# Landings of two kinds of transfers counted later by a margin in a list scheduler's order

## The chip, the cores and the metric

The kernel runs on one core of a Trainium2 chip. The metric is the device time of one execution in microseconds (us), as the median of several runs. A core has five engines that matter here, each working through its own instruction stream in order: PE (matmuls, with its weight loads shown apart as PEld), DVE, ACT, POOL and SP. SP computes nothing in this kernel; it issues all the transfers (DMAs). Engines wait for each other, and for landed transfers, by semaphores.

## The reference

Four layers are applied in turn to a batch of 128 sequences of 64 tokens and 128 features. Three have causal (or plain) self-attention, cross-attention to a second input of the same shape, and an MLP; layer 1 has cross-attention with rotary positions alone. All attention has 16 heads of 8 features. Cut to what matters:

```python
def layer(x, ctx):                                   # layers 0, 2 and 3, norms before or after
    q, k, v = split_heads(ln(x) @ w_qkv)             # 16 heads of 8 features
    x = x + merge(softmax(q @ k.T * scale) @ v) @ w_o1 + b_o1
    q, (k, v) = split_heads(ln(x) @ w_q), split_heads(ctx @ w_kv)
    x = x + merge(softmax(q @ k.T * scale) @ v) @ w_o2 + b_o2
    return x + gelu(ln(x) @ w_fc1 + b_fc1) @ w_fc2 + b_fc2

def layer1(x, ctx):                                  # rotary positions on q and k
    q, k = rope(rms(x) @ w_q), rope(ctx @ w_k)
    return x + merge(softmax(q @ k.T * scale) @ (ctx @ w_v)) @ w_o

y = layer3(layer2(layer1(layer0(x, ctx), ctx), ctx), ctx)
```

## The kernel before

**Tiling and stages.** The 8192 tokens are 16 groups of 512 tokens (8 sequences), and a group is two halves of 4 sequences. Ten stages follow each other: self-attention, cross-attention and MLP of layer 0; the cross-attention of layer 1; the three of layer 2; the three of layer 3. Each stage runs over the 16 groups. x stays in on-chip memory throughout.

**One group of an attention stage.** POOL and DVE normalize x (`xn`), PE transposes it, and PE projects queries and keys into the tile `qk`, which ACT or DVE copies out of the banks of the matmul memory (in layer 1 POOL also rotates it: four instructions, lines 719 and 721). Then `plan_spread` places it: four DMAs of 128 KB (line 761) write the keys and the queries of the group into `wide`, a buffer that is zero elsewhere, so that one matmul of 32 rows works on four heads at once. This is the transfer *wide*; the scores of the group's first half are its first reader. For each half PE computes the scores (line 850), DVE takes the maximum of each row (line 877, three instructions), POOL splits the maxima into three bf16 terms (lines 905 to 908), PE turns them (line 914), ACT copies them into `ms` (line 922), and one DMA places them into `mr` (line 918). This is the transfer *mr*. Three halves later (`LAG = 3`) PE computes the transposed scores with minus the row maxima from `mr` added, ACT takes the exponentials `e` (line 885), PE averages the values with them (line 940), and ACT or DVE copies the averages into `a`. `plan_divided` then moves `a` into `z` by two pairs of DMAs (line 961, *z*), gathers the sums of the exponentials (964, *sums*), inverts them on DVE (981), and brings them back by two DMAs (967, *inv*, and 970, *spread*). POOL divides (975, `oT`), PE projects (1030) and DVE adds to x (1015).

**The order.** The order on every engine is made while the program is built, by a list scheduler, `Plan.order`. Each step is a part with an engine, a length in us, what it reads and writes, and a due time. PE's parts have due times written by hand and are run strictly in the order of these. Every other part gets its due time from its successors, backward: the earliest due time of what comes after it, less the time between, less its own length (`length`). For a DMA the length has, besides the time to issue, a landing time and a margin `lag`:

```python
def length(self, p):
    return p.us + p.lag + (self.DMA_LAG + p.kb / self.KB_US if p.engine == "SP" else 0.0)
```

Then the scheduler plays the plan forward in its own clock: whenever an engine is free it takes, of the parts that are ready, the one due first. A DMA's readers become ready when it has landed in that clock; `kb / KB_US` is its time on the shared transfer clock:

```python
if engine == "SP":
    dma_at = max(dma_at, end) + p.kb / self.KB_US
    end = dma_at + self.DMA_LAG + p.lag
```

`DMA_LAG` is 2.4 and `KB_US` 350. Without a margin a *wide* (2.5 to issue, 512 KB) counts 6.36 us from its first issue and an *mr* (0.87 to issue, 60 KB) 3.44 us. Other DMAs have margins already: 1.0 for *z* and *inv*, 1.5 for *spread*, 4.0 for *sums*. What comes out is only an order on each engine and a choice of banks. On the chip, no time of the plan is kept: every instruction starts when its engine reaches it and its semaphores are there. SP's stream stops at a DMA whose source is not ready, and everything behind it on SP stops too.

Of the kernel before, what the change touches and what calls it, by code (L numbers as in the profile page):

```python
# [56 lines left out]
CLEAR_V = 17.0, 26.0  # L57
WARM = (16, -25.0),
GATHER = 4.0
GAP = 2.6  # L60


# [34 lines left out]
    qx=3, kx=2, v=2, mr=3, mt=2,  # L97
# [21 lines left out]
class Plan:  # L119
# [22 lines left out]
    def add(self, engine, us, run, reads=(), writes=(), fresh=(), form=None, kb=0, lag=0.0, ahead=0.0, at=None, n=0, begin=0.0, or_=None):  # L142


        p = Part(engine, us, run, self.block, form)
        p.due = None if at is None else self.begins[max(0, self.block)] + at
        assert (at is None) == (engine != "PE")
        p.fresh, p.kb, p.lag, p.ahead, p.n, p.begin, p.or_ = tuple(fresh), kb, lag, ahead, n, begin, or_
        for b in reads:
            p.before.update(b.writers)  # L150
        for b in writes:
            p.before.update(b.writers, b.readers)
        for b in reads:
            b.readers.append(p)
        for b in writes:
            if b.readers:
                b.writers, b.readers = [], []
            b.writers.append(p)
        for b in (*reads, *writes):
            if b.kind:  # L160
                b.users.add(p)
        p.before.discard(p)
        for q in p.before:
            q.after.append(p)
        self.parts.append(p)
        return p
# [160 lines left out]
def kernel(ctx, tc, x, ctxT, mask, w0, w1, w2, w3, f0, f2, f3, cols, rows, consts, factors, out):  # L327
# [11 lines left out]
    def make(b, shape, dtype, name):  # L339
        if b.kind in IN_BANKS:  # L340
            at = banks[:, b.bank:b.bank + IN_BANKS[b.kind]].rearrange("p b x -> p (b x)")
            at = (at.bitcast(dtype) if dtype != F32 else at)[:, :int(np.prod(shape[1:]))]
            dims = "abcd"[:len(shape) - 1]
            b.t = at.rearrange(f"p ({' '.join(dims)}) -> p {' '.join(dims)}", **dict(zip(dims, shape[1:])))
        else:
            b.t = pools[b.kind].tile(shape, dtype, tag=b.kind, name=name)
        return b.t
# [45 lines left out]
    add = plan.add  # L393
# [5 lines left out]
    WIDE, VBDS, MRS = ([Buf() for _ in range(n)] for n in (BUFS["kx"] + BUFS["qx"], BUFS["v"], BUFS["mr"]))  # L399
# [3 lines left out]
    def wt(n, name):  # L403
        start = W_KEPT[n].index(name) * P
        return ws[n % 2][:, start:start + W_COLS[n][name]]

    def kept(n, name):
        return W[n % 2][W_KEPT[n].index(name)]
# [124 lines left out]
    def plan_mask(name, sees, reads):  # L533
# [22 lines left out]
        add("DVE", 0.5, lay_out, reads, [mt_, by_query], [mt_, by_query])  # L556
        add("PE", 0.3, turn, [mt_, IDENT], [pm], [pm, by_key], "full", at=-11.0 if name == "causal" else GAP, n=2)
        add("DVE", 0.3, lambda: nc.vector.tensor_copy(by_key.t, pm.t[:, 0:SEQ]), [pm], [by_key])
        add("PE", 0.6, put, [by_query, by_key, PICKS], [pb], [pb], "full", at=-10.0 if name == "causal" else GAP + plan.HALF, n=12)
        add("DVE", 0.8, keep, [pb, IDENT], [MASKS[name]])  # L560
# [177 lines left out]
    def place_of(kind):  # L738

        planned[kind] += 1  # L740
        return (planned[kind] - 1) % BUFS[kind]

    def next_of(kind):
        i = counts[kind] % BUFS[kind]
        counts[kind] += 1
        return i

    def plan_spread(both, k, q):

        kx, qx, placed = Buf("kx"), Buf("qx"), Buf()  # L750

        def place():
            i, j = next_of("kx"), BUFS["kx"] + next_of("qx")
            kx.t, qx.t = wide[:, i], wide[:, j]
            row = wide.ap[0][0]
            for h in range(NQ):
                to = bass.AP(
                    tensor=wide.tensor, offset=wide.offset + h * row + i * NQ * GT + h * GT,
                    ap=[[NQ * row, QUART], [(j - i) * NQ * GT, 2], [1, GT]],
                )  # L760
                nc.sync.dma_start(to, both.t[h::NQ])  # L761

        laid = [WIDE[place_of("kx")], WIDE[BUFS["kx"] + place_of("qx")]]
        add("SP", 2.5, place, [k, q, both, *laid], [placed, kx, qx], [kx, qx], kb=512)
        return kx, qx

    def quarter(k, rows=QUART):
# [46 lines left out]
    def plan_pair(new, old):  # L814
# [74 lines left out]
        if new:  # L889
            plan.block = new.block  # L890
            plan_maxima(new)
# [4 lines left out]
    def plan_maxima(f):  # L896

        d, mt, pmx, ms = Buf("d"), Buf("mt"), Buf("m"), Buf("ms")

        def split():  # L900
            mt.t = mts[next_of("mt")]
            make(d, [P, NU, NK, NQ], F32, "d")
            terms = mt.t[:, 0:3 * HEADS * NU].rearrange("p (t k i h) -> p t k i h", t=NU, k=NK, i=3)
            to = [terms[:, :, :, i] for i in range(3)]
            nc.gpsimd.tensor_copy(to[0], f.mx.t)  # L905
            nc.gpsimd.tensor_tensor(d.t, f.mx.t, to[0], ALU.subtract)
            nc.gpsimd.tensor_copy(to[1], d.t)
            nc.gpsimd.tensor_tensor(to[2], d.t, to[1], ALU.subtract)

        def turn():  # L910
            make(pmx, [P, NU, P], BF16, "pmx")
            make(ms, [3 * HEADS, TU], BF16, "ms")
            for t in range(NU):
                nc.tensor.transpose(pmx.t[:, t, :], mt.t[:, 3 * HEADS * t:3 * HEADS * t + P], ident_b)  # L914

        def place():
            f.mr.t = mrs[next_of("mr")]
            nc.sync.dma_start(f.mr.t[0:R_LAST + 1:R_STEP], ms.t)

        add("POOL", 1.1, split, [f.mx], [mt, d], [mt, d])  # L920
        add("PE", 0.15, turn, [mt, IDENTB], [pmx], [pmx, ms], "full", at=(f.u + 1) * plan.HALF + GAP - 0.2, n=4)
        add("ACT", 0.27, lambda: nc.scalar.copy(ms.t, pmx.t[0:3 * HEADS].rearrange("p t q -> p (t q)")), [pmx], [ms])  # L922
        add("SP", 0.87, place, [ms, MRS[place_of("mr")]], [f.mr], [f.mr], kb=60)

    def plan_averages(f):

# [25 lines left out]
    def plan_divided(a):  # L952
# [3 lines left out]
        def move(part):  # L956

            if part[0] == 0:
                make(z, [P, 4, TU], F32, "z")
            for i in part:  # L960
                nc.sync.dma_start(z.t[i * QUART:(i + 1) * QUART], a.t[:, i].rearrange("p u t -> p (u t)"))
# [15 lines left out]
        for part in ((0, 1), (2, 3)):  # L977
            add("SP", 1.25, lambda part=part: move(part), [a], [z, moved], [z] if part[0] == 0 else [], kb=256, lag=1.0)
        add("SP", 0.65, gather, [moved], [sums, gathered], [sums], kb=32, lag=GATHER)
        z.users.add(plan.parts[-1])  # L980
# [55 lines left out]
    def plan_value_bias(i):  # L1036
# [6 lines left out]
        def fold():  # L1043
# [4 lines left out]
        add("PE", 0.5, lambda: nc.tensor.matmul(  # L1048
            make(pb, [P, P], F32, "pb"), bv.t, wt(3, f"wo{i}"), start=True, stop=True), [bv, kept(3, f"wo{i}")], [pb], [pb], "full", at=GAP, n=4)
        add("DVE", 0.4, fold, [pb], [ROW[f"L3_bo{i}"]])  # L1050

    def plan_attention(s, g):
        n, src = s["layer"], None
        if s["cross"]:
            src = Buf("ctx")
            add("SP", 0.45, lambda: nc.sync.dma_start(
                make(src, [P, GT], F32, "ctx"), ctxT[:, g * GT:(g + 1) * GT]), writes=[src], fresh=[src], kb=256, begin=LATER)
        hT = plan_hidden(s, g, s.get("bo"), plan.when(*plan.TURN))
        src = src or hT
        bias = lambda name: col_put[:, B_PUT.index(s[name]):B_PUT.index(s[name]) + 1] if name in s else None  # L1060
        a, both = Buf("a"), Buf("qk")
        k = plan_operand(0, both, n, s["wk"], src, "rope" in s, bias("bk"), pad if s["mask"] == "cross" else None)
        q = plan_operand(1, both, n, s["wq"], hT, "rope" in s, bias("bq"), sees_any[:, 0] if s["mask"] == "self" else None)
        kx, qx = plan_spread(both, k, q)
        begun.append(kx)
        vbd = plan_values(s, src)
        block = plan.block
        given = [MASKS[s["mask"]], IDENTB] if s["mask"] else []
        for u in range(NU):
            f = types.SimpleNamespace(  # L1070
                s=s, g=g, u=u, block=block, mask=s["mask"], both=both, kx=kx, qx=qx, vbd=vbd, a=a,
                given=[k, q, *given], mx=Buf("mx"), mr=Buf("mr"), es=[Buf("e"), Buf("e")],
            )
            halves_on.append(f)
            plan_pair(f, halves_on.popleft() if len(halves_on) > LAG else None)
# [309 lines left out]
```

## Time and profile before

| | us |
|---|---|
| three runs | 1709.56, 1715.78, 1714.78 |
| median of the three | 1714.78 |
| the profiled execution, its own time | 1710.07 |
| its span, first to last instruction | 1708.1 |

The stages take these stretches of the span, with the busy time of some engines (from a table of windows; the borders are read from the first and last matmuls of each stage, to a few us):

| stage | stretch, us | length | PE busy | POOL busy | DMA share |
|---|---|---|---|---|---|
| layer 0 self | 22 to 222 | 200 | 188.10 | 132.81 | 0.46 |
| layer 0 cross | 222 to 394 | 172 | 165.94 | 110.83 | 0.52 |
| layer 0 MLP | 394 to 520 | 126 | 124.43 | 84.65 | 0.14 |
| layer 1 cross | 520 to 704 | 184 | 175.43 | 143.23 | 0.47 |
| layer 2 self | 704 to 909 | 205 | 197.31 | 109.61 | 0.42 |
| layer 2 cross | 909 to 1087 | 178 | 173.39 | 145.59 | 0.51 |
| layer 2 MLP | 1087 to 1226 | 139 | 132.60 | 123.41 | 0.14 |
| layer 3 self | 1226 to 1406 | 180 | 173.28 | 145.45 | 0.39 |
| layer 3 cross | 1406 to 1579 | 173 | 168.61 | 118.85 | 0.53 |
| layer 3 MLP | 1579 to 1708 | 129 | 123.49 | 61.60 | 0.21 |

How to read the views shown below: the view of waits has one line for each pair of waiter and releaser ("who, which line, waited for whom: us in total, times, longest"). The chain of waits is followed back from the last instruction, at each step to what released it. The timeline gives start, length, engine and line, and in brackets the idle time before. "q" after an engine's name is its sequencer, so SPq L918 is the issue of the *mr* transfer.

### The profile page before, as it was taken

Reading aid. Unit: us, or ns where it says so; the run is one execution under the profiler, and the core shown is the slowest. Engines: PE = TensorE matmul, PEld = TensorE weight load, DVE = VectorE, ACT = ScalarE, POOL = GpSimd, SP = SyncE. Lnnn points to the kernel's source line nnn. Section 1 sums busy time; section 2 is a strip of 40 time slices with the busy share of each in tenths; the row PEclk is TensorE's granted clock in tenths of the full one; section 3 lists DMA queues with packets and bytes.
Section 4 is the critical chain, followed back from the end, with each engine's and each line's share of the span. In section 5 each row is a group of like instructions: output and inputs, shape, how many; then the busy total and the mean of one; then the engine's idle time right before and its main releaser. Section 6 shows DMA issues by size and latency. Waiting matters only on the chain.

```text
span 1708.1 us, 87778 instructions
## 1 busy us (share of the span) xinstructions
PE 1638.8 (96%) x38243; PEld 1258.5 (74%) x38243; DVE 1162.2 (68%) x2758; ACT 1198.7 (70%) x1789; POOL 1186.0 (69%) x1912
## 2 busy tenths in 40 slices
PE   7999999999999999999999999999899999999999
PEld 4677777767996676777777766799667777777898
DVE  7667676675557777556666767566799987778452
ACT  7777777877445777777777777844387877777643
POOL 4666766666768887436558886899778887657570
PEclk9999999999999999999999999999899999999999
DMA  4444355553003455544444555310124445554311
GB/s 148 131 141 138 115 149 147 152 158 80 13 11 102 135 154 149 146 120 122 118 124 134 147 154 143 92 28 7 45 98 133 134 133 146 156 162 141 72 45 44
DMA packets 194624, 195.05 MB, mean 114 GB/s; under 512 B 53952, under 2 KB 142144, under 8 KB 194240
## 3 DMA queue, kind: packets, MB, share of 16 engines
q1 hardware_dynamic: 194240, 189.45, 38.4%
q8 instruction: 300, 4.92, 1.3%
q14 instruction: 84, 0.69, 0.1%
HBM read 25.51 MB, written 4.19 MB: 17 GB/s over the span
## 4 chain that ended last, share of the span: by engine, by line
PE 73%; POOL 6%; DVE 6%; DMA 5%; issue 3%; ACT 3%; SPq 3%; POOLq 0%; DVEq 0%; ACTq 0%
PE banks L850 26%; PE banks L940 11%; PE banks L704 9%; PE banks L1121 8%; PE banks L1108 6%; PE banks L1030 5%; PE banks L997 4%; PE banks L653 3%; DVE mx L877 3%; PE banks L914 2%; ACT e L885 2%; DMA wide<-qk 2%; DMA mr<-ms 2%; POOL xn L620 1%; SPq L761 1%
## 5 line engine op out<-in xcount | busy, mean ns | idle before, releaser
L877 DVE TENSOR_REDUCE mx<-banks 128x8 f32<-128x512 f32 (+1 forms) x672 | 548.6, 861 | 256.6 <-PE banks L850 245.9
L850 PE MATMUL banks<-wide,qk 32*64 32x256 f32 x14336 | 540.1, 381 | 21.9 <-issue 16.0
L885 ACT ACTIVATE e<-banks 128x512 f32<-128x512 f32 (+1 forms) x576 | 391.6, 739 | 149.3 <-PE banks L850 146.6
L850 PEld LDWEIGHTS banks<-wide,qk 32*64 32x64 f32 x14336 | 346.6, 132 | 92.6 <-issue 36.8
L940 PEld LDWEIGHTS banks<-e,v 128*32 128x32 f32 x14336 | 212.8, 110 | 102.8 <-issue 79.6
L1002 ACT COPY v<-banks 64x512 f32<-64x512 f32 x224 | 247.1, 1103 | 33.0 <-PE banks L997 31.4
L940 PE MATMUL banks<-e,v 128*32 128x64 f32 x14336 | 250.1, 221 | 6.4 <-ACT e L885 5.5
L684 POOL TENSOR_TENSOR x<-x,row_sb 128x512 f32<-128x512 f32 x144 | 185.4, 1293 | 54.4 <-PE banks L653 52.3
L1113 ACT ACTIVATE h<-banks,col_sb 128x512 f32<-128x512 f32 x192 | 126.3, 688 | 120.4 <-PE banks L1108 82.5
L1121 PEld LDWEIGHTS banks<-w,h 128*128 128x128 f32 x1536 | 190.6, 192 | 15.3 <-issue 3.9
L1121 PE MATMUL banks<-w,h 128*128 128x128 f32 x1536 | 197.5, 276 | 3.2 <-ACT ms L922 3.1
L947 ACT COPY a<-banks 128x512 f32<-128x512 f32 x221 | 129.5, 586 | 95.6 <-PE banks L940 92.4
L620 POOL TENSOR_TENSOR xn<-x,mv 128x512 f32<-128x512 f32 x109 | 118.0, 1083 | 99.0 <-PE banks L653 93.3
L975 POOL TENSOR_TENSOR oT<-z 128x512 f32<-128x512 f32 x112 | 144.0, 1285 | 51.9 <-DMA z<-inv 17.1
L613 POOL TENSOR_TENSOR rstd<-rstd,nhalf 128x4 f32<-128x4 f32 x160 | 166.9, 1043 | 13.4
L704 PE MATMUL banks<-turned,wp 128*128 128x512 f32 x320 | 163.5, 604 | 2.7 <-ACT turned L578 1.7
L905 POOL CAST mt<-mx 128x32 bf16<-128x32 f32 x224 | 47.5, 212 | 145.9 <-DVE mx L877 143.8
L598 DVE BATCH_NORM_STATS2 st<-x 128x6 f32<-128x128 f32 x640 | 139.0, 277 | 10.7 <-POOL x L664 5.2
L850 PE MATMUL banks<-mr,minus 32*64 32x512 bf16 x1280 | 129.4, 388 | 5.1 <-DMA mr<-ms 4.5
L1030 PE MATMUL banks<-w,oT 128*128 128x128 f32 x896 | 119.4, 276 | 1.2 <-issue 1.2
L620 POOL TENSOR_TENSOR xn<-xn,rstd 128x512 f32<-128x512 f32 x109 | 115.3, 1058 | 5.7
L1030 PEld LDWEIGHTS banks<-w,oT 128*128 128x128 f32 x896 | 109.5, 192 | 2.8 <-issue 1.3
(121 smaller groups left out, 2563.3 us busy)
## 6 DMA issues: line engine op xcount, KB each, us to landing
wide<-qk SPq DMA_DIRECT2D x448, 128.0 KB
z<-a SPq DMA_DIRECT2D x448, 128.0 KB
z<-inv SPq DMA_DIRECT2D x112, 256.0 KB
ctx<-in_ctxT_dram SPq DMA_DIRECT2D x64, 256.0 KB
mr<-ms SPq DMA_DIRECT2D x224, 24.0 KB
x<-in_x_dram SPq DMA_DIRECT2D x16, 256.0 KB
out_dram<-x SPq DMA_DIRECT2D x16, 256.0 KB
sums<-z SPq DMA_DIRECT2D x112, 32.0 KB
```

The costliest lines, as they stand in the source:

```text
L613: nc.gpsimd.tensor_tensor(r, r, nhalf, ALU.pow)
L620: nc.gpsimd.tensor_tensor(xn.t, xg if step == 0 else xn.t, by_, ALU.subtract if mean else ALU.mult)
L684: add("POOL", 1.28, lambda: nc.gpsimd.tensor_tensor(xg, xg, row(out_bias), ALU.add), [ROW[out_bias]], [X[g]])
L704: nc.tensor.matmul(a.t, w, src.t, start=True, stop=True)
L850: nc.tensor.matmul(m[0], m[1], m[2], start=m[3], stop=m[4])
L877: add("DVE", (1.15 if step else 0.61), lambda b=b, k=k, n=2 // len(sc[step]): nc.vector.tensor_reduce(new.mx.t[:, :, k:k + n].rearrange("p ...
L885: add("ACT", 0.5 if n == 1 else 0.95, lambda b=b, to=e, n=n, i=i: nc.scalar.activation(to.t[:, i:i + n].rearrange("p i h n q -> p (i h n q ...
L940: nc.tensor.matmul(av.t[j * VO:(j + 1) * VO, i, h * SEQ:(h + 1) * SEQ], f.vbd.t[:, 2 * f.u + h, v], f.es[i // 2].t[:, i % 2, h, j], start= ...
L975: nc.gpsimd.tensor_tensor(oT.t.rearrange("p t c q -> p c t q"), x, r, ALU.mult)
L1002: copy(vbd.t[half, :, :, c::4], pv.t[half])
L1030: nc.tensor.matmul(po.t[:, t, :], oT.t[:, t].rearrange("p c q -> p (c q)"), wo, start=True, stop=True)
L1121: nc.tensor.matmul(po.t[:, t, :], hs[k // 2].t[:, k % 2, t * P:(t + 1) * P], fc2[:, k * P:(k + 1) * P], start=k == t == 0, stop=k == NC4 - ...
```

## The change

A constant is added, and the two `add` calls that plan *wide* and *mr* get it as their margin. Nothing that is computed, no transfer and no buffer is changed.

```diff
 GATHER = 4.0
+PLACE = 1.5
 GAP = 2.6
@@ plan_spread
-        add("SP", 2.5, place, [k, q, both, *laid], [placed, kx, qx], [kx, qx], kb=512)
+        add("SP", 2.5, place, [k, q, both, *laid], [placed, kx, qx], [kx, qx], kb=512, lag=PLACE)
@@ plan_maxima
-        add("SP", 0.87, place, [ms, MRS[place_of("mr")]], [f.mr], [f.mr], kb=60)
+        add("SP", 0.87, place, [ms, MRS[place_of("mr")]], [f.mr], [f.mr], kb=60, lag=PLACE)
```

The length counted for a *wide* becomes 7.86 us and for an *mr* 4.94 us, so both and what feeds them are due 1.5 us earlier, and in the plan's clock their readers are ready 1.5 us later.

The two built programs have the same instructions, and compared engine by engine their orders stand so (groups are numbered 0 to 111 over the seven attention stages, 16 to a stage; "a" and "b" are a group's halves):

| engine | difference |
|---|---|
| PE | none: 11266 rows (equal neighbours merged) in both, in the same order; the banks that the tiles take are others |
| ACT | one swap in the first 20 us (a clearing of a buffer goes ahead of the copy of a transposed x) |
| SP, start | a 256 KB and a 64 KB load of weights move ahead of the *mr* of half 1a, a 0.5 KB load of biases ahead of the *wide* of group 3; ahead of the *wide* of group 4 small loads change places |
| SP, layer 0 self | ahead of the *wide* of groups 7 to 12, `x mr` becomes `mr x` (x is the load of a later group's input, 256 KB) |
| SP, layer 0 cross | ahead of the *wide* of groups 24 to 31, `mr sums z inv ctx mr z spread` or `mr z inv sums ctx mr z spread` becomes `mr inv z sums ctx mr spread z` |
| SP, layer 1 | between two *wide*, `z mr inv mr ctx sums z spread` becomes `mr z inv sums mr ctx z spread` ahead of the *wide* of groups 39, 41, 43 and 45, and stays in those between; once (group 39) a second *mr* goes ahead of the *wide* |
| SP, layer 2 | ahead of the *wide* of groups 56 to 79 as in layer 0 cross |
| SP, layer 3 | none, up to the last group's tail |
| DVE | in most groups of layer 2 and some of layers 0 and 1 the inversion (981) comes after the third maximum of a half (877) or ahead of line 1015, where it stood one place off; in places means and variances (598, 603) move past one or two neighbours |
| POOL, layers 0 cross and 2 cross | in 22 groups the division `oT` moves ahead of one or both steps of `xn` (620), with one reciprocal root (612, 613) past a split of the maxima in some; in four groups of layer 2 self ahead of a reciprocal root |
| POOL, layer 1 | the reciprocal roots (608 to 613) of later groups, which stood ahead of the rotations (719, 721) in groups 38 to 42, are earlier by some groups or stand behind the rotations |
| POOL, layer 3 | one `xn` step moved at the end of the cross-attention |

## The prediction

> **What bounds the kernel now.** I read the busy times first, then the chain of waits, then the waits stage by stage, and last the SP queue beside PE in one group.
>
> ```profile
> span 1708.1 us, 87778 instructions
> PE 1638.8 (96%) x38243; PEld 1258.5 (74%) x38243; DVE 1162.2 (68%) x2758; ACT 1198.7 (70%) x1789; POOL 1186.0 (69%) x1912
> ...
> PE 73%; POOL 6%; DVE 6%; DMA 5%; issue 3%; ACT 3%; SPq 3%; POOLq 0%; DVEq 0%; ACTq 0%
> ```
>
> PE is busy for 1638.8 of 1708.1 us, and its instructions and their order stay as they are. What the change can win is therefore within the 69.3 us in which PE stands, and only the part of it that waits on *wide* and *mr* is aimed at. Over the whole span the view of waits has:
>
> ```profile
> PEld L850 <- DMA mr<-ms: 10.9, 17, 1.7
> ...
> PE banks L850 <- DMA wide<-qk: 4.5, 9, 1.1
> PE banks L850 <- DMA mr<-ms: 4.5, 6, 1.3
> ```
>
> 9.0 us of standing matmuls and 10.9 us of standing weight loads, which overlap in part: 9 to 20 us. A second way to size it: for the first matmul of each half that reads a newly landed *wide* or *mr*, I took from the timeline the time since the matmul before it, less that of an undisturbed half of the stage. That gives by stage: layer 1 6.0 us on *mr* and 1.3 on *wide*; layer 0 cross 1.7 and 1.6; layer 3 cross 1.9 and 2.6; about 2 in the rest. Together 17 us, 1.0% of the run, and this is the ceiling. The same waits in the window of layer 1 (520 to 704):
>
> ```profile
> PE banks L850 <- DMA mr<-ms: 2.7, 4, 1.2
> ...
> PEld L850 <- DMA mr<-ms: 6.8, 10, 1.7
> ```
>
> More than a third of the ceiling lies in this one stage of 184 us. Why, one of its groups shows (chain of waits):
>
> ```profile
> 648.89 1.28 SPq L761
> ...
> 651.56 0.58 SPq L961
> ...
> 652.83 3.51 DMA mr<-ms
> 656.34 0.04 issue
> 656.38 2.13 PE banks L850 x63
> ```
>
> The maxima were in `ms` at 646.74 (end of ACT's line 922), but SP was first busy with *wide* (648.21 to 651.5, it had waited for POOL's rotation) and a pair of *z*, so *mr* went out at 652.83, 6.1 us later, and PE took it 0.04 us after it landed. In layer 1, 11 of 32 *mr* are met within 0.2 us of landing, all of the b halves; the median from `ms` to issue is 2.96 us and from issue to landing 2.45. In layer 3 cross 8 of 32 are that tight (median to issue 3.43), in layer 0 cross 2, in layer 2 none: there the median slack from landing to use is 4.4 to 4.6 us.
>
> **The change, part by part.** It adds no work: 448 and 224 DMAs stay, each as large. All it does is the other order.
>
> *Layer 1, where the waits are.* In every second group *mr* b passes one pair of *z*, 1.23 us of issue in the rows above (651.56 to 652.83), and often a short wait of that pair for `a`. The *mr* concerned stand, by my per-half list, for 0.09, 0.88, 0.32, 0.21 and 1.62 us; each becomes shorter by at least 1.2 us, so 0.09 + 0.88 + 0.32 + 0.21 + 1.2 = 2.7 to 3.1 us go. The other tight b halves (0.44, 0.50, 0.73, 0.09, 0.92, 0.32: 3.0 us) keep their place behind *z*. They can gain through POOL: *wide* waits for the rotations, and the reciprocal root that stood ahead of these costs 8.3 + 1.8 + 1.6 + 1.6 = 13.3 us for 8 groups, 1.66 us each. In some five groups it is now off that path, which brings *wide*, *z* and *mr* forward by up to 1.66 us. Ends: 0 (something else holds the rotations) and 3.0 + 1.3 (all that is left of both kinds). I take 2.5, nearer the upper end, since the chain in this stage runs through POOL, rotations and *wide*. Together 2.9 + 2.5 = 5.4 us off. What is late next is the exponentials (line 940 waits for ACT 2.3 us there) and the maxima (0.4). Passed over are the *z* pair and *sums*, later by one *mr*, 0.87 us; `oT` is ready 4.9 us or more before PE reads it in this stage, which covers it. Once an *mr* goes ahead of a *wide* whose slack was 0.38 us: 0.87 − 0.38 = 0.5 us back.
>
> *Layer 0 cross and layer 2.* *inv* and *spread* each pass other DMAs, *sums* and one *z* pair fall back. *mr* and *wide* have as many DMAs ahead of them as before, and so keep their times: the waits of layer 0 cross (3.3 us) stay, and layer 2 had 0.3 (one *wide*). I take 0. On POOL `oT` is now ahead of two steps of `xn` (1083 and 1058 ns). In layer 2 cross it began a median 2.48 us after *spread* had landed; 2.14 of that go, and *spread*, issued ahead of a *z* pair, comes 1.2 us sooner: it still fits. `xn` falls back by the 1285 ns of `oT`; its transposes come 6 us or more after it in most groups of layer 2 cross and 6.9 in layer 0 cross: covered. The third maximum is up to 541 ns sooner (the inversion's length), but a split of the maxima is done 1.9 to 3.6 us before PE turns it, so it gains nothing.
>
> *Layer 0 self and the start.* `mr x` for `x mr` brings *mr* forward by one issue of x (0.51 us) or its wait (up to 1.77), in a stage with one tight *mr*: nothing. x lands 0.85 us later for 6 groups; DVE has waited for it 3.6 us in 4 places. Ends 0 and 6 × 0.85 = 5.1; DVE is busy for 65% of the stage, so I take 1.0 back. At the start 320 KB pass the *mr* of half 1a: two issues (0.33 to 0.63 us each) and 320 KB at the 148 GB/s of that slice, 2.2 us, together some 3.2, less its slack of 2.34: 0.9 back at most. A mask load that DVE was held up by (the chain has 3.43 us of it, ending at 52.29) is issued one or two places sooner, 0.6 to 1.3. I take 0.
>
> *Layer 3 and the MLPs.* SP is the same, so its 4.5 us of tight landings stay: 0.
>
> **Where a rule speaks against it.** By the rows of this trace an *mr* lands 2.0 us after its issue at the least, 2.06 to 3.04 as the stages' medians, 6.79 at most; a *wide* lands 5.3 to 6.0 us after its first issue (medians), 7.25 at most. The plan counted 3.44 (2.57 of it after the issue) and 6.36 already, so the margin fits the worst landings and not the usual ones. The Trainium skill, "DMA: Bandwidth & Descriptors", section "Anatomy of one DMA", fits a DMA by a fixed cost of about 2.0 us and its bytes over 436 GB/s (for another issuing path). By it a margin has nothing to cover and the sum would be 0; by the rows the time lost is ahead of the issue, in the queue, which only a changed order mends, and the sum is what layer 1 gives.
>
> **The sum.** −5.4 + 0.5 + 1.0 = −3.9, with the smaller *wide* waits left as they are: about −4 us. The profiled execution took 1710.07 (span 1708.1 and 2.0 around it), below the median of the three, 1714.78; the difference carries over to the median: 1714.78 − 4 = 1710.8. The ends of this case: −8 (−5.4 − 1.8 more in layer 1, −0.8 of the mask load) and 0 (2.7 in layer 1 less 0.5, 1.0 and 0.9), so 1707 to 1715.
>
> **Rivals.** *More goes than I see.* `mr` 5.4 in layer 1 with all of its 7.3, the 3.3 of layer 0 cross if *wide* there stops waiting behind a *spread* that waits for *inv* (it went out as little as 0.02 us after *inv* had landed), and some of the 8.4 us in which line 914 waits for DVE, of which 1.7 are in layer 0 cross and 3.5 in layer 0 self: 7.3 + 3.3 + 2 to 5 = −13 to −16, 1699 to 1702. For it: the same order in every group of layer 2 and a POOL that is freer. Against: layer 3 keeps its waits.
>
> *Given back.* x, the start and the *wide* behind an *mr* cost 1.0 to 5.1, 0.9 and 0.5, and layer 1 gives only 2.7: −0.3 to +3.8, 1714.5 to 1718.5.
>
> *Slower: instruction blocks arrive later.* The profile has
>
> ```profile
> q8 instruction: 300, 4.92, 1.3%
> ...
> PE banks L850 <- issue: 19.0, 25, 3.3
> ```
>
> 300 blocks of 16 KB are fetched by the DMA engines that carry the data, and at nearly every one of these 25 waits a block had landed 1.2 to 1.6 us before PE went on: PE runs out of instructions. Layer 2 self has 6.7 us of it in 9 waits, layer 2 cross 2.8 in 4. There *spread* (256 KB), a *z* pair (256 KB) and *wide* (512 KB) follow each other in another order, and fetches may meet them worse. If each of the 24 changed groups of layer 2 and the 8 of layer 0 cross lost one such wait of 0.75 us (6.7 / 9) it would be 24.0, against 9.5 + 1.2 now: +13, and with layer 1's gain +9 to +13, 1724 to 1728. It decides from some 12 more waits. Against it: the bytes between two *wide* stay the same. The skill's "Runtime: NRT & Kernel Launch", section "Instruction fetch mechanics", calls fetching hidden by the dispatch; by it this rival would be 0, but the row of 19.0 us disagrees.
>
> *The margin does nothing.* PE's order is the same, and layer 3 shows that whole stages stay; it goes with "given back".
>
> **How the numbers follow.** Forecast 0.46 (0.05 of it under −8.6), more 0.24, given back 0.14, slower 0.16. 0.5% of the median is 8.6 us, about what a measurement of this kernel can tell from no change (its three runs span 6.2). Faster by more: 0.05 + 0.24 = 0.29; within: 0.41 + 0.14 = 0.55; slower: 0.16. The range 1698 to 1722 takes in the forecast, nearly all of "more" and "given back", and leaves out most of "slower"; the forecast's own is 1707 to 1715.
>
> **What would show it.** In layer 1's window the PEld row on *mr* falls from 6.8 us to under 4, its stretch from 184 to about 179; layer 3's waits on *mr* and *wide* (0.6, 2.2 on PE; 2.3 on PEld) stay as they are; layers 0 cross and 2 stay within 2 us each; `oT` does not wait longer for *spread*. I am wrong if layer 1 keeps its waits, or if layer 2 moves by more than 3 us in either direction.

## The result and the profile after

| | before | changed |
|---|---|---|
| runs on the same chip | 15 | 15 |
| median, us | 1709.52 | 1718.80 |
| range, us | 1703.81 to 1715.78 | 1712.76 to 1728.11 |
| the profiled execution, us | 1710.07 | 1722.72 |
| its span, us | 1708.1 | 1720.9 |

The changed kernel is slower: the ratio is 1.0052, with a 95% interval of 1.0037 to 1.0068, or 9 us where I forecast 4 us less. The range of 1698 to 1722 holds the time, partly by luck: it was laid around 1714.78, the median of three runs, and the fifteen have 1709.52. The direction was wrong.

The changed kernel's line numbers are one higher than before's (L851 for L850, L919 for L918). The first lines of its page and of its chain:

```profile
span 1720.9 us, 87771 instructions
PE 1640.7 (95%) x38243; PEld 1262.0 (73%) x38243; DVE 1164.3 (68%) x2758; ACT 1198.8 (70%) x1789; POOL 1186.1 (69%) x1912
...
PE 72%; POOL 8%; DMA 5%; DVE 4%; issue 4%; SPq 4%; ACT 3%; POOLq 0%; DVEq 0%; ACTq 0%
```

PE's work is the same (1640.7 against 1638.8 us); it stands 80.2 us instead of 69.3. Whole-run waits of PE and PEld:

```profile
PE banks L851 <- issue: 18.3, 21, 3.6
PE banks L915 <- DVE mx L878: 12.2, 11, 3.9
PE banks L851 <- DMA mr<-ms: 7.6, 13, 1.1
PE banks L851 <- DMA wide<-qk: 7.3, 8, 1.7
...
PEld L851 <- DMA mr<-ms: 14.9, 17, 1.5
```

The waits that the margin was aimed at grew: *mr* from 4.5 to 7.6 us, *wide* from 4.5 to 7.3, the weight loads' from 10.9 to 14.9. The waits for DVE grew from 7.3 to 12.2. The fetch of instructions (19.0 before) did not grow in this pair.

PE runs the same 38243 matmuls in the same order in both, so the traces can be laid on each other matmul by matmul. A stretch below runs from the first matmul that before started in it to the first of the next:

| stretch of before, us | before | changed | difference |
|---|---|---|---|
| start and layer 0 self, 0 to 222 | 220.2 | 221.5 | +1.4 |
| layer 0 cross, 222 to 394 | 172.0 | 181.1 | +9.1 |
| layer 0 MLP, 394 to 520 | 126.1 | 126.1 | 0.0 |
| layer 1, 520 to 704 | 184.0 | 189.8 | +5.8 |
| layer 2 self and cross, 704 to 1087 | 383.1 | 382.2 | -0.9 |
| layer 2 MLP, 1087 to 1226 | 139.0 | 135.7 | -3.3 |
| layer 3, 1226 to the end | 477.7 | 478.1 | +0.4 |

Together 12.5 of the 12.8 us between the spans. The loss sits in two stages, and three findings in the trace name its pieces.

**Layer 0 cross: SP.** The waits of PE and of PEld in this stage (223 to 404 us of the changed execution):

```profile
PE banks L851 <- DMA wide<-qk: 4.6, 3, 1.7
PE banks L851 <- DMA mr<-ms: 3.2, 6, 1.1
...
PEld L851 <- DMA mr<-ms: 6.3, 7, 1.5
```

Before had 1.4, 1.3 and 1.7 there. Why they land later, SP's timeline shows for one group, from one *wide* to the next:

```profile
373.43 3.76 SPq L762 DMA_DIRECT2D wide<-qk  x4
377.29 0.83 SPq L919 DMA_DIRECT2D mr<-ms  x1
378.22 0.58 SPq L968 DMA_DIRECT2D inv<-sums  x1
378.91 1.73 SPq L962 DMA_DIRECT2D z<-a  x2
380.69 0.59 SPq L965 DMA_DIRECT2D sums<-z  x1
381.38 0.83 SPq L919 DMA_DIRECT2D mr<-ms  x1
382.31 1.59 SPq L971 DMA_DIRECT2D z<-inv  x1
383.95 1.42 SPq L962 DMA_DIRECT2D z<-a  x2
385.48 3.10 SPq L762 DMA_DIRECT2D wide<-qk  x3
```

Before had for the same group:

```profile
364.54 2.57 SPq L761 DMA_DIRECT2D wide<-qk  x4
367.21 0.90 SPq L918 DMA_DIRECT2D mr<-ms  x1
368.21 0.58 SPq L964 DMA_DIRECT2D sums<-z  x1
368.88 1.25 SPq L961 DMA_DIRECT2D z<-a  x2
370.22 0.56 SPq L967 DMA_DIRECT2D inv<-sums  x1
370.87 1.55 SPq L918 DMA_DIRECT2D mr<-ms  x1
372.48 1.22 SPq L961 DMA_DIRECT2D z<-a  x2
373.80 0.58 SPq L970 DMA_DIRECT2D z<-inv  x1
374.56 3.69 SPq L761 DMA_DIRECT2D wide<-qk  x4
```

From one *wide* to the next it is 10.02 us before and 12.05 changed. There is no rest between the changed rows beyond the 0.05 to 0.11 us from one issue to the next: SP is always issuing or standing at an issue whose source is not there. A *wide* takes 2.57 when nothing holds it, a pair of *z* 1.23, *spread* 0.58; in the changed rows they take 3.76, 1.73 and 1.42, and 1.59. To see what that leaves, I counted each issue between the *wide* of group 24 and that of group 31 at the shortest length usual for its kind (the lower tenth: 0.59 for one of the four of *wide*, 0.81 *mr*, 0.58 one of *z*) and called the rest of it a wait. Per group before: 8.50 of issues, 1.30 between them, 1.23 of waits, 11.03 in all. Changed: 8.50, 1.15 and 2.69, 12.34 in all. A group that PE runs undisturbed takes 10.72 in this stage. So SP needs 9.7 of 10.7 us for its issues and the time between them, and the room for waits is about 1 us per group.

**Layer 1: a load of weights.** The chain of waits around the longest stall of the stage:

```profile
668.28 3.48 DMA put<-in_w_dram
671.77 0.02 issue
671.79 0.04 DVE wp L439
...
672.25 0.61 DVE mx L878
672.86 0.04 issue
672.90 0.37 PE banks L915 x2
```

SP issues the two loads of layer 2's weights (`put`, line 429 of before) some 8 us later in relation to PE than before (667.69 against 646.85 us, of which 12.8 are the delay of all), on the other side of a *wide*. DVE keeps the place of the copy that reads them, stands there 4.7 us, and the maxima behind it are late: PE stands 3.9 us.

**Layer 1: a root.** The chain 125 us earlier, where PE stands 1.8 us:

```profile
546.64 1.04 POOL rstd L614
547.67 0.18 POOL mt L906
...
548.85 0.40 PE banks L915 x2
```

A reciprocal root (545.74 to 547.68) now stands ahead of the split of the maxima. It left the way of the rotations, as the prediction had it, and got into another.

**Behind the stalls: the clock.** The rows of layer 1, before and changed (stretch, length, busy time of PE, PEld, DVE, ACT and POOL with their instructions, granted clock, DMA share, GB/s):

```profile
520.00:704.00 184.00, 175.43 (x4552) 124.69 (x4550) 137.65 (x267) 130.86 (x200) 143.23 (x244) 1.00 0.47 137
530.00:720.00 190.00, 176.57 (x4553) 126.24 (x4553) 138.22 (x267) 131.24 (x200) 143.11 (x244) 0.97 0.46 133
```

In the changed execution the granted clock is 0.50 from 548.6 to 552.0 and from 671.4 to 678.2 us, right behind the two stalls, and full in the rest of the stage; before has it full throughout. Half of these 10.2 us, 5.1, is an estimate of the matmul time lost; against it and the stalls stands the weight loads' wait for *mr*, which fell by 2.8 us. In layer 0 cross one such stretch follows a wait for *wide* (391.6 to 395.0; 1.7 of the 9.1 us by the same estimate). In the MLP of layer 2 before has one (1201.1 to 1207.9; 3.4 us) and the changed kernel none. Over the twenty traces, 109 of 110 such stretches begin right behind 3.4 us in which PE was busy for at most 0.7. A long stall of PE can cost more than its own length here.

### The profile page after: what moved, and what is told of

Its sections match the earlier page's. It is cut to its first block, busy times and chain, and to the rows that moved or that the text cites. A ratio compares the mean times of both kernels' runs of the same rounds, so it can differ in the third digit from the quotient of the medians.

```text
span 1720.9 us, 87771 instructions
## 1 busy us (share of the span) xinstructions
PE 1640.7 (95%) x38243; PEld 1262.0 (73%) x38243; DVE 1164.3 (68%) x2758; ACT 1198.8 (70%) x1789; POOL 1186.1 (69%) x1912
## 4 chain that ended last, share of the span: by engine, by line
PE 72%; POOL 8%; DMA 5%; DVE 4%; issue 4%; SPq 4%; ACT 3%; POOLq 0%; DVEq 0%; ACTq 0%
PE banks L851 25%; PE banks L941 11%; PE banks L705 9%; PE banks L1122 7%; PE banks L1109 5%; PE banks L998 5%; PE banks L1031 5%; PE banks L654 3%; PE banks L915 2%; DMA mr<-ms 2%; ACT e L886 2%; POOL xn L621 2%; SPq L762 2%; DVE mx L878 2%; DMA wide<-qk 1%
## 5 line engine op out<-in xcount | busy, mean ns | idle before, releaser
L851 PE MATMUL banks<-wide,qk 32*64 32x256 f32 x14336 | 541.9, 381 | 27.0 <-issue 15.5
L851 PEld LDWEIGHTS banks<-wide,qk 32*64 32x64 f32 x14336 | 348.3, 131 | 94.2 <-issue 36.6
L851 PE MATMUL banks<-mr,minus 32*64 32x512 bf16 x1280 | 130.0, 390 | 8.5 <-DMA mr<-ms 7.6
```

The source lines that it names most:

```text
L851: nc.tensor.matmul(m[0], m[1], m[2], start=m[3], stop=m[4])
```

## The experiments

Most of them are hybrids. The kernel plans twice, with the margin at 0 and at 1.5, which gives `old` and `new`, the lists of steps of each engine. It then builds the list `take` of each engine from the two and plays the plan a third time with every engine but PE, whose order is fixed, bound to its list. `as_in(a, b, part)` keeps the places that the steps of `part` have in `a` and fills them in the order of `b`; `between(sp, i, j)` are SP's steps from *wide* number i to number j, counted from 0. The hybrids keep before's line numbers. Ratios are to before on the same chip, with 95% intervals. Stage lengths are of one profiled execution each, by the matmuls of the table above, and several executions with the same order in a stage serve as one another's measure. A few diffs below are sketches of SP's order ahead of one *wide*, written with the names of the transfers.

### SP's order in layer 0 cross

Into before, and out of the changed kernel (`b_sp`, `a_sp`):

```diff
 take = dict(old)
+take["SP"] = as_in(old["SP"], new["SP"], between(old["SP"], 23, 33))
```
```diff
 take = dict(new)
+take["SP"] = as_in(new["SP"], old["SP"], between(new["SP"], 23, 33))
```

> The orders of before on every engine, and of the change only SP's order between the wide of group 23 and that of group 33 (layer 0 cross). Theory A (in this stage SP itself is nearly full, and 'mr inv z sums ctx mr spread z' makes it wait longer, so mr and wide land later): the stage goes from 172.0 us to 179 to 182, the run becomes 7 to 10 us longer than before (ratio 1.004 to 1.006), and the other stages stay within 2 us. Rival B (the order of POOL or DVE in that stage, or the other banks of the matmul memory, made the loss): the stage stays at 171 to 174 and the run within 2 us of before.

> The orders of the changed kernel on every engine, except SP's order between the wide of group 23 and that of group 33, which is that of before. Theory A: layer 0 cross goes back from 181.1 us to 171 to 174 and the run loses 7 to 10 us, to a ratio of 0.999 to 1.002 to before. Rival B (POOL, DVE, banks): the stage stays near 181 and the ratio near 1.005.

`b_sp`: 178.7 us for the stage, ratio 1.0026 (1.0001 to 1.0051). `a_sp`: 174.0, ratio 1.0035 (1.0012 to 1.0058). The stage follows SP's order both ways, 6.7 us in and 7.1 out; the whole follows it by about half of that, within the intervals, and both ratios lie outside what theory A expected.

The two pieces of that order, each alone (`b_spr`, `b_inv`; in some of the groups before has `z inv sums` for `sums z inv`):

```diff
-mr sums z inv ctx mr z spread WIDE
+mr sums z inv ctx mr spread z WIDE
```
```diff
-mr sums z inv ctx mr z spread WIDE
+mr inv z sums ctx mr z spread WIDE
```

> The orders of before; of the changed order only one piece, in layer 0 cross ahead of the wide of groups 24 to 31: spread goes ahead of the pair of z that it followed. Theory A1 (the harm is here: the pair of z, which waits for the averages, now stands directly ahead of wide): layer 0 cross from 172 to 177 to 181 us. Theory A2 (the harm is in inv ahead of z and sums): the stage at 171 to 174.

> The orders of before; of the changed order only the other piece, ahead of the wide of groups 24 to 31: 'mr inv z sums ctx mr' for 'mr sums z inv ctx mr' or 'mr z inv sums ctx mr', with z spread as before. Theory A2: layer 0 cross from 172 to 176 to 181 us; theory A1: 171 to 174. If both pieces cost some 3 us, the harm is in each place that SP stops.

`b_spr`: 179.3 us, ratio 1.0041 (1.0016 to 1.0066). `b_inv`: 176.2, ratio 1.0007 (0.9982 to 1.0033). The swap of *spread* and *z* is enough for the whole loss; the other piece shows 3 us over the mean of before's order in the stage (see below) and nothing that can be told in the total.

Is it that SP is full? `b_load` adds issues to before in a full stage and in a freer one, `a_act` takes one off SP in the changed kernel:

```diff
     for p in plan.order():
         p.run()
+        wides += p.kb == 512
+        if p.engine == "SP" and (p.kb == 512 or p.kb == 256 and p.us == 0.65) and (wides in range(25, 33) or wides in range(57, 65)):
+            more = 8 - more
+            nc.sync.dma_start(pads[:, more:more + 8], rows[:, more:more + 8])
```
```diff
-            add("SP", 0.45, lambda: nc.sync.dma_start(
+            add("SP", 0.45, lambda: (nc.scalar if n == 0 and g in range(7, 16) else nc.sync).dma_start(
```

> Before, with two more tiny loads (32 bytes each, some 0.55 us of SP and 0.1 between) after each wide and each spread of groups 24 to 31 (layer 0 cross) and 56 to 63 (layer 2 self). Theory A (in layer 0 cross SP works 9.8 us of a group whose floor on PE is 10.7, in layer 2 self 9.1 of 12.4): layer 0 cross gets 3 to 10 us longer (at most 8 x 1.3), layer 2 self stays within its spread of 2 us. Rival (SP has room everywhere, what counts is only which wait stands ahead of what): both within 2 us.

> The changed kernel, with the loads of ctx for groups 23 to 31 (layer 0 cross) issued by ACT instead of SP: some 0.55 us and a wait of up to 1.8 us less on SP in each group, and the changed order of all other issues kept. Theory A (SP is full there and late, and everything that it issues is late with it): layer 0 cross goes from 177 to 181 us (four executions with this order) to 172 to 176, and fewer mr are met at their landing. Rival (it is the pair of z directly ahead of wide that waits, whatever else SP does): the stage stays at 177 to 181.

`b_load`: layer 0 cross 179.8 us, layer 2 self 202.7 where twelve executions with before's order there have a mean of 202.6; ratio 1.0029 (1.0002 to 1.0057). Two loads of 32 bytes per group cost over 6 us in one stage and nothing in the other. `a_act`: 175.3, against 177.4 to 181.1 with the changed order on SP. Its waits of PE in the stage:

```profile
PE banks L850 <- ACT a L947: 2.1, 4, 0.7
PE banks L850 <- DMA wide<-qk: 1.1, 1, 1.1
PE banks L850 <- DMA mr<-ms: 1.0, 1, 1.0
```

*wide* and *mr* wait 1.1 and 1.0 us in place of 4.6 and 3.2, and 2 of 32 *mr* are met within 0.2 us of landing where the changed kernel has 12; ACT, which now issues, gives 2.1 back. Over the whole run no gain shows (1.0053, 1.0027 to 1.0079; one of 4 us would lie at the edge of this): layers 1 and 2 keep the changed order and were long in the profiled execution (190.8 and 389.5).

So theory A holds, with one limit. Twelve executions with before's order on SP in this stage have 169.7 to 177.7 us (mean 173.4), and two of the twelve are as long as the changed ones (177.4 to 181.1, mean 178.7, four executions). Before's order can fall behind as well; the changed order does so each time.

Much of that width is one group's. From the fourth to the fifth output projection of the stage (271.8 to 285.0 us of before), where SP's order is the same in all but `a_act`, the twenty executions take 12.2 to 16.9 us, whatever order follows. Without it the stage has 157.0 to 163.5 (mean 159.5) with before's order and 161.7 to 167.2 (mean 163.3) with the changed one, 164.7 in `b_spr`, 167.5 in `b_load`, but 160.2 in `b_inv` and 159.3 in `a_act`. So the 3 us of `b_inv` are not its piece's, one issue less per group on SP brings the stage back whole (one execution each), and the changed order costs nearer to 4 us than to 5.

### Layer 1

The loads of weights back at their places (`a_w`):

```diff
-z mr inv mr ctx sums z spread WIDE44 ... sums put put mr ctx z spread put put WIDE45
+z mr inv mr ctx sums z spread put put WIDE44 ... sums put put mr ctx z spread WIDE45
```

> The orders of the changed kernel, except that the two loads of layer 2's weights (put, line 429) are back at their old places on SP in layer 1, ahead of the wide of group 44 instead of behind it. Theory A2 (DVE stands at line 438 until the load has landed, and the maxima behind it with it): the wait of 4.2 us ahead of line 914 near 670 us goes, layer 1 goes from 189.8 us to 185.5 to 187, and the run becomes 3 to 4.5 us shorter than the changed kernel (ratio to before 1.002 to 1.004). Rival: the wait is only seen in this execution, or the maxima are late for another reason: layer 1 stays at 189 to 191 and the ratio at 1.005.

Layer 1 took 183.3 us, at full granted clock; PE no longer waits for DVE's maxima in the stage. The changed order with the loads at their new places has 185.2, 189.8 and 190.8 (`a_sp`, the changed kernel, `a_act`; mean 188.6). Ratio 1.0040 (1.0017 to 1.0062): the stage is as expected and better, the total at the edge of it, with layer 0 self at its longest in this execution (226.3 to its end).

SP's order alone, and POOL's alone, in stages that lie apart (`b_l0_l1`, `b_pool_l2`):

```diff
 take = dict(old)
+for lo, hi in ((1, 13), (36, 46)):
+    take["SP"] = as_in(take["SP"], new["SP"], [p for p in between(old["SP"], lo, hi) if p.kb != 128])
```
```diff
 take = dict(old)
+take["POOL"] = as_in(old["POOL"], new["POOL"], [p for p in old["POOL"] if 49 <= p.block < 65])
+take["SP"] = as_in(old["SP"], new["SP"], between(old["SP"], 55, 79))
```

> The orders of before, with SP's order from the changed kernel in two stages that lie apart: ahead of the wide of groups 3 to 12 (layer 0 self) and of groups 37 to 45 (layer 1), the weight loads left where they were. Layer 1: if SP's order alone brings the gain seen between 600 and 660 us (58.8 to 60.6 us for that stretch in before's order, 56.1 to 57.8 with the changed order), that stretch takes 56 to 58 and the stage some 3 us less than 184; if the roots' places on POOL bring it, 60 and 184. Layer 0 self: with before's order six executions took 196.9 to 201.2 us, with the changed one three took 201.2 to 205.9; if SP's order does that, 201 to 206, if not, 197 to 201.

> The orders of before, with two pieces of the changed one in stages that lie apart: POOL's order in layer 1 (a reciprocal root goes ahead of the split of the maxima in the first groups) and SP's order in layer 2 ahead of the wide of groups 56 to 79 (the same swaps as in layer 0 cross). Layer 1: line 914 waits 1.6 to 1.9 us for POOL early in the stage, which gets that much longer in its first 20 us. Layer 2: by theory A (mr and wide have 4 us of slack here, and SP is less full) self and cross stay within 2 us of the means of before's order, 203.3 and 176.0; by the rival (the swaps cost wherever they are made) each gets 5 us or more longer.

`b_l0_l1`: layer 1 took 183.9 us (before's order: 183.4 to 186.7, mean 184.7, ten executions), the stretch of 600 to 660 us some 2 less than the mean of before's order and the 20 us behind it 1.4 more. Up to 222 us it took 219.4: SP's `mr x` costs nothing. Ratio 0.9999 (0.998 to 1.0018). SP's order in layer 1 alone brings no gain that can be told. `b_pool_l2`: layer 1 took 188.1, and its waits have

```profile
PE banks L914 <- POOL mt L908: 3.7, 3, 1.8
```

where before has 0.4. POOL's order costs 3 us in layer 1 beside before's order on SP (188.2 in `b_eng`, below). Beside the changed order on SP it does not: `a_w` has it, with 2.3 us of these waits, and took 183.3. So the two orders are not worth what each is worth alone; these are single executions.

### Layer 2

`b_pool_l2` has 383.6 us for layer 2 self and cross, and a ratio of 1.0043 (1.0024 to 1.0063). That is neither the 2 us of theory A nor the 10 of its rival. So its two pieces were taken apart, the same swaps as above, ahead of the *wide* of groups 56 to 79:

> Before, and in layer 2 ahead of the wide of groups 56 to 79 spread goes ahead of the pair of z. Layer 2 self and cross together took 374 to 383 us (mean 377.7) in nine executions with before's order there, 382 to 386 (mean 383.2) in five with the changed one. If this swap does it: 382 to 386, with PE's waits for instructions in layer 2 self at 6 to 10 us (3.8 to 6.9 with before's order); if not, 374 to 380.

> Before, and in layer 2 ahead of the wide of groups 56 to 79 the other piece, inv ahead of z and sums. If this does it: self and cross together 382 to 386 us, PE's waits for instructions in layer 2 self 6 to 10; if not, 374 to 380. If both pieces stay low, the loss needs both.

`b_l2_spr`: 383.8 us, ratio 1.0027 (1.0004 to 1.005). `b_l2_inv`: 388.1, ratio 1.0041 (1.002 to 1.0062). `b_eng`, below, with before's order on SP and run with them: 379.2. Over all profiled executions the two stages took 377.8 with before's order (374.0 to 383.1, twelve) and 384.2 with the changed one (382.2 to 389.5, six). Before's own profiled execution is the longest of its twelve, which is why the pair above shows nothing here. The pieces alone stand 5 and 9 us above `b_eng`. In the twelve, PE waits for instructions 3.8 to 7.3 us in layer 2 self (mean 5.7), in the six 5.8 to 9.5 (mean 8.0): 2.3 of the 6.4 us. The waits of `wide_only` (before's order on SP there) and of `b_pool_l2` in that stage:

```profile
PE banks L850 <- issue: 3.6, 8, 0.9
```
```profile
PE banks L850 <- issue: 7.8, 9, 1.6
```

`b_l2_spr` has only 5.4 of it, though, with its loss in layer 2 cross, where 5.1 us of landings of *mr* stand. `b_l2_inv` has 5.2, and 3.2 and 3.5 us of waits of line 850 for ACT's line 947 in the two stages. So each execution loses in another place, and what the rest is made of is not settled.

### Each margin alone

```diff
-        add("SP", 2.5, place, [k, q, both, *laid], [placed, kx, qx], [kx, qx], kb=512, lag=PLACE)
+        add("SP", 2.5, place, [k, q, both, *laid], [placed, kx, qx], [kx, qx], kb=512)
```
```diff
-        add("SP", 0.87, place, [ms, MRS[place_of("mr")]], [f.mr], [f.mr], kb=60, lag=PLACE)
+        add("SP", 0.87, place, [ms, MRS[place_of("mr")]], [f.mr], [f.mr], kb=60)
```

The first is `mr_only`, the second `wide_only`.

> The margin on mr alone. By the built order SP goes in layers 0 cross and 2 as in the changed kernel and the weight loads of layer 2 stay where before had them, the first pair ahead of the wide of group 44. Theory A: layer 0 cross 177 to 181 us, layer 1 within 3 us of 184, the run 1.002 to 1.005 of before. Rival (the two margins act together, or wide's is the harmful one): layer 0 cross near 172, the run within 2 us of before.

> The margin on wide alone. By the built order SP goes in layer 0 cross as before, and the weight loads of layer 2 go out a group later as in the changed kernel. Theory A: layer 0 cross 171 to 174 us; in layer 1 DVE stands for the weights and line 914 waits 2 to 4 us near 660 us, the stage 185 to 188; the run 1.000 to 1.004 of before. Rival (each margin does the whole harm): layer 0 cross near 179.

`mr_only`: layer 0 cross 177.5, layer 1 183.7, layer 2 385.5 us; ratio 1.0025 (0.9991 to 1.0058). `wide_only`: layer 0 cross 169.7, layer 1 186.0, layer 2 374.6; ratio 0.9991 (0.9972 to 1.001). The margin on *mr* is what turns SP's order round in layers 0 cross and 2. That on *wide* moves the loads of weights (DVE stood 2.8 us for them, PE 1.6) and costs nothing that can be told. Layer 0 cross and the total of `wide_only` came out below what theory A expected, and the interval of `mr_only` still holds no change.

### The other engines, the banks, and the best of both

`b_banks` is before in every order, with the banks of the margin's clock; `b_eng` has the changed orders on DVE, ACT and POOL and before's on SP; `b_eng_l0` and `b_eng_l2` have these only in layer 0 self and only from layer 2 on; `best` takes what seemed good.

```diff
-return play(plan, 0.0, old)
+return play(plan, PLACE, old)
```
```diff
-take = dict(new)
+take = dict(new, SP=old["SP"])
```
```diff
 take = dict(old)
+for e in ("DVE", "ACT", "POOL"):
+    take[e] = as_in(old[e], new[e], [p for p in old[e] if p.block < 17])
```
```diff
 take = dict(new)
+take["POOL"] = as_in(new["POOL"], old["POOL"], [p for p in new["POOL"] if 49 <= p.block < 65])
+take["SP"] = as_in(old["SP"], new["SP"], [p for p in between(old["SP"], 36, 46) if p.kb != 128])
```

> The orders of before on every engine, but the banks of the matmul memory chosen in the plan's clock with the margin counted, so that most matmul outputs lie where the changed kernel has them. Theory A (only orders matter): within 2 us of before, every stage within 2 us. Rival C (the other banks, by letting ACT or DVE hold PE up, made part of the loss): up to 1.005, with layer 0 cross or layer 1 3 us or more longer.

> SP's order of before, the changed orders on DVE, ACT and POOL, and their banks. Theory: layer 0 cross 170 to 175 us, layer 2 374 to 380, layer 1 1.9 us longer at its start for the root on POOL (186 to 188), the stretch from 1087 to 1226 at 136 to 137.5 instead of 138.8; the run within 0.998 to 1.002 of before. Rival (the other engines' orders make part of the loss beyond layer 1): 1.003 or more, seen in a stage's length.

> Before, with the changed orders of DVE, ACT and POOL among the steps of layer 0 self alone. If the moved statistics and maxima on DVE cost the time there: the stretch up to 222 us takes 222 to 226 us (nine executions with before's orders: 218.8 to 221.6), the run some 2 to 5 us more than before, 1.001 to 1.003. If the longer executions were the clock's or the fetches' doing: 219 to 222, and within 0.999 to 1.001.

> Before, with the changed orders of DVE, ACT and POOL from layer 2 on, SP's as before. Theory: the stretch from 1087 to 1226 takes 136.5 to 137.5 us instead of 138.7, layer 2 374 to 380, all else as before: 1 to 3 us under before, a ratio of 0.998 to 1.000, which would make it the fastest version, by less than can be told with certainty. Rival: 1.001 or more.

> What the runs say is good in the changed order, alone: its orders on DVE and ACT, on POOL outside layer 1, and SP's order ahead of the wide of groups 37 to 45 with the weight loads at their old places; SP elsewhere and POOL in layer 1 as before. Theory A: layer 0 cross 171 to 174, layer 1 181 to 183, the stretch from 1087 to 1226 2 to 3 us shorter than before's 138.8: 4 to 7 us under before, a ratio of 0.996 to 0.998. Rival (the gains come only together with the losses): 0.999 to 1.002.

`b_banks`: 1.0004 (0.9981 to 1.0027), no stage over 1 us longer than in before: the banks are not it. `b_eng`: 1.0011 (0.9987 to 1.0036), 224.0 us up to the end of layer 0 self. `b_eng_l0`: 223.6 there, 1.0019 (1.0001 to 1.0036): the moved statistics and maxima cost 3 us, as far as can be told (before's orders 218.8 to 221.6, mean 220.1, eleven executions; these orders 221.5 to 226.3, mean 223.9, seven). Of the 3.8 between the means, 2.7 go with the granted clock: stretches at 0.50 cost an estimated 5.8 us in the seven and 3.1 in the eleven. Whether the orders bring these stretches on is not shown. `b_eng_l2`: PE's wait for line 1045 in the MLP of layer 2 is 1.6 us, as with these orders in all eight executions that have them there (1.6 to 1.8) and in none of the twelve others (4.6 to 4.7). The stage took 138.2 all the same, above what I expected, with the granted clock at 0.50 in its last 5 us; ratio 1.0003 (0.998 to 1.0025). `best`: 1.003 (1.0009 to 1.005), slower than before, against my expectation; it kept the orders that `b_eng_l0` shows to cost (225.6 up to 222). No version was shown to be faster than before.

The stages' means do not add up to the whole: 3.8 (layer 0 self), 5.3, 3.9 (layer 1), 6.4 and −2.0 (MLP of layer 2) make 17 us, and the medians of fifteen runs differ by 9.3 (6.3 to 11.6). The profiled executions show where time goes, and not its shares.

## Why the prediction was wrong

**The step that failed.** "*mr* and *wide* have as many DMAs ahead of them as before, and so keep their times" in layers 0 cross and 2, priced at 0. The number of DMAs ahead is the same; how long SP stands at them is not, and I did not count how full SP was. In layer 0 cross it is full to about 1 us per group, and a stall in a full queue is passed on to all behind it. It cost 9.1 us in the pair, 5.3 in the means of sixteen executions, 3.8 without the group that no moved issue reaches. In layer 2 I called the landings covered by 4.4 to 4.6 us of slack; the means say 6.4 us lost, of which 2.3 are the fetch of instructions; what the rest is stays open.

**Layer 1, -5.4 + 0.5.** The mechanism was there: the weight loads that wait for *mr* fell from 6.8 to 4.0 us. But PE's own wait fell only from 2.7 to 2.1, and three things stood up in its place: the root ahead of a split (PE's wait on POOL 0.4 to 2.3), the load of weights (3.9), *wide* (0.6 to 1.9). Behind the first two the granted clock was 0.50 for 10.2 us, some 5 us by the estimate above, and the sum had no term for that. The 2.5 that I gave to roots moved out of the rotations' way is a loss of some 3 in `b_pool_l2` (none in `a_w`): I named where the roots left and not where they went. The load of weights moved past a *wide* I did not price at all: DVE has a fixed place for what reads it.

**Layer 0 self, +1.0 for x behind *mr*.** SP's swap costs nothing (`b_l0_l1`), yet 3 to 4 us are lost, with the order on DVE, ACT and POOL (`b_eng_l0`; 1.4 in the pair), much of it as granted clock. I had looked at DVE's moved statistics and given them no price.

**Layer 3 as before.** Right: +0.4 us.

**The MLP of layer 2.** Not in the sum, and 3.3 us shorter in the pair, 138.7 to 136.7 in the means: PE's wait for DVE's line 1045 falls from 4.7 to 1.6 us, as the load of layer 3's weights goes out sooner, and the stretch at half clock behind the longer wait (3.4 us by the estimate) is gone; 1.4 come back as a wait of line 850 for DVE. It comes with the orders of DVE, ACT and POOL (`b_eng_l2`), not with SP's (4.6 in `b_pool_l2`). Which of their moved steps does it was not found.

**The rivals.** "Given back" had the direction, with at most 3.8 of the 9 us, and not the places: x behind *mr* cost nothing. The one on the slower side, more fetches that come late, is about a third of what happened in layer 2 and next to none of it in layer 0 cross (1.5 us before, 1.8 changed). "The margin does nothing" and "more goes" are out.

**The rule on fetches.** The Trainium skill's "Runtime: NRT & Kernel Launch", section "Instruction fetch mechanics", calls them mostly hidden. By their number they are, with 25 waits before at 300 blocks; but they are 19.0 us of PE's standing before and 18.3 after, and in layer 2 self they vary from 3.8 to 9.5 between executions. For SP another rule bears: "DMA: Bandwidth & Descriptors", section "Issuing engines are not separate DMA queues", says that issuing from a second engine saves only the sequencer's time, usually small beside the DMA. One issue is small here too, 0.55 to 0.82 us beside 2.0 or more to landing; but the issues of a group add up to 9.7 of 10.7 us, so in layer 0 cross the sequencer's time is the scarce thing, and one issue less per group brought the stage back (`a_act`).

## What to carry to other kernels

Before a reorder is priced, add up what the issuing queue does in one period: issues, the time between them, waits. If it comes near the period of the engine that bounds the kernel, that queue is a second bound, and an order is judged by which stall it puts ahead of which transfer, not by how many transfers. Follow each moved step to its new neighbours: what it now holds up costs as surely as what it no longer holds up. Look at the granted clock behind each long stall before pricing the stall.

A margin in a list scheduler is a change of every order that hangs on it: here the one on *mr* turned the queue round in layers 0 cross and 2 and lost time in both.

## What the runs showed of the hardware

The granted clock falls early in the run, and not in each execution alike: between 40 and 70 us before had a mean of 0.83 and `b_l0_l1` 0.94, with the same orders on PE, DVE, ACT and POOL. The windows of before:

```profile
22.00:40.00 18.00, 14.47 (x355) 9.94 (x354) 9.77 (x27) 12.52 (x17) 9.67 (x22) 1.00 0.56 184
40.00:70.00 30.00, 26.76 (x756) 20.21 (x758) 19.22 (x53) 20.42 (x32) 20.14 (x32) 0.83 0.41 125
```

The columns are as in the rows of layer 1 above. Later in the run it falls behind long stalls of PE, as told there. And the same order on SP leaves a stage a width of its own: 374.0 to 383.1 us for layer 2 self and cross in twelve executions of kernels that have before's order on SP there, so a single pair of profiles can hide, or make, an effect of 6 us. The MLP of layer 0 took 126.1 us in all twenty.
